# Seven small moves at the passage from projections to attention in a sparse graph attention layer

## The chip, the cores and the metric

The kernel runs on one core of a Trainium2 chip. The metric is the device time of one execution in microseconds (us); less is better. A core has TensorE (PE) for matrix products, VectorE (DVE), ScalarE (ACT) and GpSimd (POOL) for the rest, and a queue processor SyncE (SP). SP, ACT and POOL issue DMA transfers; the indirect ones (gathers and scatters by row numbers) are issued by POOL.

## The reference

One layer of graph attention over 4096 nodes of width 512, 8 heads of 64, then a feed-forward network and a last norm. The adjacency matrix is 4096 x 4096 of int32 and sparse: some 17 neighbours a row, the node itself among them.

```python
hs = layer_norm(x);  ht = layer_norm(h_target)           # with scale and bias, masked
q = (ht @ Wq + bq) / 8;  k = hs @ Wk + bk;  v = hs @ Wv + bv
logits = einsum('thd,shd->hts', q, k); logits = where(adj != 0, logits, -1e30)
ctx = einsum('hts,shd->thd', softmax(logits), v)
ht = layer_norm(ht + ctx @ Wo + bo)
out = _layernorm(x + ht + gelu(ht @ W1) @ W2)
```

## The kernel before

Rows lie in 32 tiles of 128. The kernel turns each adjacency row into a list of neighbours, sorts the rows by the number of neighbours so that rows of like degree share a tile, and then gathers the k|v rows of the neighbours. It has two stages.

*Stage 1* weaves three streams. `projections` normalizes x, multiplies it by Wk and Wv (L947, 16 pairs of tiles, n = 0 to 15) and writes each tile's k|v rows to a table in DRAM, `kvd` (L953, issued by ACT). Beside it `late_constants` makes small constants, one step at each n from 4 on; its last step, at n = 8, is a product of `rbc` and `wq` (L668) that corrects q's bias row `bqr` (L670, L671). `prepare` makes the lists of the first 16 adjacency tiles, part A: each quarter of a tile (512 KB) is loaded on SP (L714), turned into bytes by ACT (Sign, L733) and searched by DVE (L740, L742). Then `sort(0)` ranks the rows and POOL scatters the list records into DRAM (L871). `first_fronts` begins q for the first two (`EARLY`) sorted tiles. `fill` makes the lists of 7 further tiles (`FILL`).

*Stage 2* weaves four streams. `attention` goes over the sorted tiles in groups of `GROUPS`: 17 groups, the first and the last of one tile, the others of two. A sorted tile has a cap of neighbours (11 for tile 0, up to 39 for tile 15), and they are taken in steps `SG` of `S` = 3 slots. For each slot POOL gathers 128 k|v rows (L985) into a place of `ring`, up to 4 steps ahead (`request`, `issue`). DVE multiplies k by q (L1239) and sums by head (L1244), ACT takes Exp (L1248, L1257), DVE and ACT weight v (L1200 for the first two slots of a step of three, L1223 for the third, L1204 adds pairs), and PE adds the slots up in PSUM (L1211). `front(i)` prepares q of a tile: gather of target rows, norm (L1017), transposes (L1021, copies L1024), product with wq (L1031), bias (L1036). `finish` ends a tile: 1/sum, product with Wo (L1132), norm (L1150), transposes into `h2T` (L1159, L1163). `feed(g)` is the FFN of a group: W1 (L1344), gelu (L1347), W2 (L1353); it sleeps while `h2T` of its group is missing. `other_lists` makes the lists of the last 9 adjacency tiles and runs `sort(1)` for part B; it starts at `WAIT`. `weights` loads two quarters of W1 and W2.

`_weave` sets the order in which the program is written down: each stream yields costs in units, and the stream with the least sum goes next; a stream that yields None sleeps until another has gone. A group of two tiles costs 60 units in attention and 60 in its feed. A scheduler of the framework then makes each engine's queue: the written order is the priority, but work that is ready and finds its engine free may go ahead. `behind(ins)` (`tc.issue_after`) queues an instruction behind another of the same engine. For that purpose `front` has the tie L1013: a DVE step that reads what stage 1 or attention wrote last (`latest`) and passes on the two factors of the norm.

`prefetch(i)` loads the record of a sorted tile, on POOL for part A and on SP for most of part B, and requires that its part has been scattered (`done`). Tile 16 is the first of part B.

The ring has 17 places for part A and 20 for part B. In stage 1 its places 0 to 7 hold adjacency quarters, 8 to 11 rows of h_target, 12 to 16 rows of x; two further places (`wide`) hold the quarters of tiles from number 22 on.

Of the kernel before, what the change touches and what calls it, by code (L numbers as in the profile page):

```python
# [443 lines left out]
def adj_resnorm_kernel(  # L444
# [43 lines left out]
    NQ = 4  # L488
# [44 lines left out]
    with tc.tile_pool(name="keep", bufs=1) as keep:  # L533
# [17 lines left out]
        with ExitStack() as late:  # L551
# [146 lines left out]
                nc.vector.bn_aggr(mv, st)  # L698


            held, moms, factors, maxima = [], list(range(NT)), [], []
            mvh = wp.tile([P, NT, 2], F32, name="mvh")

# [16 lines left out]
            def edges(i):  # L720

                part = 1 if i >= NA else 0
                rec = Rs[part][:, i - PARTS[part][0], :]
                cand = lp.tile([P, SEG, 8], U16, name="cand", bufs=2)
                for h in range(NQ):
                    n = i * NQ + h
                    while len(adjs) < min(n + 2, NT * NQ):
                        adjs.append(quarter(*divmod(len(adjs), NQ)))
                    a, adjs[n] = adjs[n], None

                    sg = turn_of("signs", signs)
                    with behind(newest if i >= NA else []):
                        nc.scalar.activation(sg, a, AF.Sign, accum_out=dpart[:, i, h:h + 1])  # L733
                    ahead = min(n + DEEP - 1, n + 3 + n // 2)
                    while len(adjs) < min(max(n + 3, min(ahead, RINGED * NQ)), NT * NQ):
                        adjs.append(quarter(*divmod(len(adjs), NQ)))
                    yield 0.0 if i < NA else 0.7 if i < NA + FILL else 1.0
                    wd = sg.bitcast(U16)
                    with behind(logits):
                        nc.vector.tensor_tensor(wd, wd, lio, ALU.mult)  # L740
                    for s, (w0, w1) in enumerate(SEGS):
                        maxima[:] = [nc.vector.max(cand[:, h * SQ + s, :], wd[:, w0:w1]).ins]  # L742
                    if h == 1:
                        keep_rest()
                    if h % 2 and moms:
                        moments(moms.pop(0))
                    yield 1.8 if i < NA else 0.7 if i < NA + FILL else 1.0
                dec = dec_w
                nc.vector.tensor_single_scalar(dec[:, 0], cand, 255, op=ALU.bitwise_and)
                nc.vector.tensor_single_scalar(dec[:, 1], cand, 8, op=ALU.logical_shift_right)  # L750
                gid = lp.tile([P, 2 * SEG, 8], F32, name="gid")
                dec = dec.rearrange("p b s e -> p (b s) e")
                off = segoff.rearrange("p b q s -> p (b q s)")
                nc.vector.scalar_tensor_tensor(gid, dec, 0.0,
                                               off.unsqueeze(2).to_broadcast([P, 2 * SEG, 8]),
                                               op0=ALU.is_gt, op1=ALU.mult)
                nc.vector.scalar_tensor_tensor(gid, dec, 2.0, gid, op0=ALU.mult, op1=ALU.add)
                flat = gid.rearrange("p s e -> p (s e)")
                for r in range(RE // 8):
                    top = rec[:, E0 + r * 8:E0 + (r + 1) * 8]  # L760
                    nc.vector.max(top, flat)
                    if r + 1 < RE // 8:
                        nc.vector.match_replace(flat, top, flat, 0.0)
                held.append((rest_d[i * P:(i + 1) * P, :], flat))
                has = lp.tile([P, MAXE], F32, name="ehas")
                nc.vector.tensor_scalar(has[:, :RE], rec[:, E0:E0 + RE], 0.0, 0.0, op0=ALU.is_gt,
                                        op1=ALU.add, accum_out=cnt[:, i:i + 1])
                yield 2.4 if NA <= i < NA + FILL else 4.0
# [45 lines left out]
            def sort(part):  # L814
# [54 lines left out]
                for i in range(n):  # L869
                    with behind(issues):  # L870
                        ins = nc.gpsimd.indirect_dma_start(  # L871
                            out=recs_d[part][:, :],
                            out_offset=bass.IndirectOffsetOnAxis(ap=ranki[:, i:i + 1], axis=0),
                            in_=R[:, i, :], in_offset=None)

                    tc.declare_no_dep(ins.ins, group=f"scatter{part}", reason="other rows")
                    tc.add_to_no_dep_group(f"scatter{part}", ins.ins)
                    yield 3.0 if part else 1.3
                done.add(part)


# [107 lines left out]
            def prefetch(i):  # L989
                if i >= NT or i in recs:  # L990
                    return
                r0 = TILES[i][0]
                part = 1 if r0 >= PARTS[1][0] * P else 0
                assert part in done
                r0 -= PARTS[part][0] * P
                rec = sp.tile([P, E0 + MAXE], I32, name="rec", bufs=6)

                (nc.sync if part and i < NT - 4 else nc.gpsimd).dma_start(rec[:, :RW], recs_d[part][r0:r0 + P, :])
                recs[i] = rec

            def front(i, idle=0):


                rec = recs[i]
                tq = sp.tile([P, 2 * D], F32, name="tq", bufs=3)
                t = tq[:, :D]
                gather(t, h_target, rec[:, TGT:TGT + 1])
                for _ in range(max(idle, 1)):
                    yield


                m = rec[:, RST:RST + 2].bitcast(F32)
                tie = nc.vector.scalar_tensor_tensor(m, m, latest[-1], m, op0=ALU.bypass,  # L1013
                                                     op1=ALU.max)
                with tc.issue_after(tie.ins):
                    nc.vector.tensor_copy(tags[:, i, :], rec[:, DEG:TGT + 1])
                nc.scalar.activation(t, t, AF.Identity, bias=m[:, 1:2], scale=m[:, 0:1])  # L1017
                yield
                pt = ps.tile([P, KC, P], F32, name="t", bufs=2)
                for kc in range(KC):  # L1020
                    nc.tensor.transpose(pt[:, kc, :], t[:, kc * P:(kc + 1) * P], ident)  # L1021
                hT = tq[:, D:].rearrange("p (c t) -> p c t", c=KC)
                for kc in range(KC):
                    nc.scalar.activation(hT[:, kc, :], pt[:, kc, :], AF.Identity,  # L1024
                                         bias=b1r[:, kc:kc + 1], scale=s1c[:, kc:kc + 1])
                yield
                yield
                yield
                pq = ps.tile([P, D], F32, name="t", bufs=2)
                for kc in range(KC):  # L1030
                    nc.tensor.matmul(pq, hT[:, kc, :], wq[:, kc, :], start=kc == 0,  # L1031
                                     stop=kc == KC - 1)
                yield
                yield
                yield
                nc.vector.scalar_tensor_tensor(tq[:, :D], pq, HD ** -0.5, bqr,  # L1036
                                               op0=ALU.mult, op1=ALU.add)
                tqs[i] = tq
# [2 lines left out]

            SG = [(i, j0, min(S, cap - j0)) for i, (_, cap) in enumerate(TILES)
                  for j0 in range(0, cap, S)]
            kvs, rests, fronts = {}, {}, {}
            place = [11]
            for i, _, n in SG:
# [29 lines left out]
            def issue(k):  # L1076
# [3 lines left out]
                        begin(SG[k + d][0], d)  # L1080
                i, j0, n = SG[k]
                if j0 == 0:
                    prefetch(i + 2)
                    begin(i, 0)
                    if TILES[i][1] > RE:
# [85 lines left out]
            def first_fronts():  # L1171
# [4 lines left out]
                    step(fronts, i)  # L1176
                while not latest:
                    yield None
                while fronts:
                    go_on()  # L1180
                    yield 4.0

            def attention():
# [143 lines left out]
                    tc.add_to_no_dep_group("out", ins.ins)  # L1327

            def feed(g):
                while g not in h2Ts:  # L1330
                    yield None
                group, h2T = GROUPS[g], h2Ts.pop(g)
                nt = len(group)
                w = nt * P
# [62 lines left out]
                for g in gens:  # L1397
                    yield from g

            WAIT = 100.0  # L1400
            AHEAD = 4
            ADDS = 11
            HEAVY = 30
# [11 lines left out]
            def projections():  # L1415
                yield from _some(proj, G)
                consts = late_constants()
                for n in range(1, both):
                    if n > 3:
                        next(consts, None)  # L1420
                    yield from _some(proj, G)
                    if n in (8, 10):
                        load_quarter(wp2, n // 2 - 4)
# [47 lines left out]
                        load_quarter(pool, q + 2, nc.scalar)  # L1471

            def other_lists():
                for cost in ed:
                    yield 2.2 * cost
                keep_rest()
# [39 lines left out]
```

## Time and profile before

| | |
|---|---|
| median of 8 runs | 1792.59 us (1788.01 to 1797.17) |
| profiled execution | 1792.79 us, span 1791.0 us |
| PE busy | 1667.8 us, 93% of the span |
| DVE, ACT, POOL busy | 1425.4, 1239.9, 1022.9 us |
| gathers of k|v rows (L985) | 603, 1.32 us of POOL each |
| DMA | 461 MB, mean 257 GB/s |
| last k|v row issued, first gather of k|v rows | 276.01 us, 281.21 us |
| first FFN matmul | 344.91 us |

Times in the profile are microseconds from the start of the span. L12 is line 12 of the kernel. A stage's row gives the length, then the busy time of PE, PE's weight loads, DVE, ACT and POOL (with instruction counts), the granted clock of TensorE, the mean busy share of the 16 DMA engines, and GB/s. A wait names who waited (engine, tile, line), for whom, the sum, how often, and the longest. "Issue" is time in which the engine waited for nothing that the profile shows. POOL has 0.3 us of it ahead of nearly every gather. fp32 products count as two PE instructions each.

### The profile page before, as it was taken

To read this page: it belongs to the slowest core of one execution; us is meant where nothing else is said; L and a number is where in the kernel's file an instruction comes from. 1 tells how busy PE (TensorE), PEld (TensorE's weight loads), DVE (VectorE), ACT (ScalarE), POOL (GpSimd) and SP (SyncE) were. 2 spreads that over 40 slices of the span, in tenths; PEclk is the share of its full clock that TensorE was granted. 3 is DMA by queue.
4 is the path that set the end of the run, shared out by engine and by line. 5 is a ranking of instruction groups with operands and counts; after the bars stand their busy time and mean duration, and the time that the engine had idled before them with its cause. 6 is when DMAs were issued, how large, how long until landed. Compare 5 with 4: busy or idle time off the path is not lost. (4 is left out here: it accounts for less than half of the span.)

```text
span 1791.0 us, 22463 instructions
## 1 busy us (share of the span) xinstructions
PE 1667.8 (93%) x6850; PEld 1079.3 (60%) x6850; DVE 1425.4 (80%) x2449; ACT 1239.9 (69%) x3133; POOL 1022.9 (57%) x822
## 2 busy tenths in 40 slices
PE   7989985798999999997989999999999999999997
PEld 3444433556666766665656766666666666666665
DVE  6887786869888888996989888999797888988500
ACT  5776663558787888765777867787787677877511
POOL 1000155657456566787787787777677767764101
PEclk9999998898999999998999999999999999999999
DMA  9999978968678787777887788877668777775000
GB/s 351 361 384 358 365 241 300 338 230 286 250 251 300 275 312 276 248 233 228 284 288 279 263 296 296 288 251 264 231 219 280 241 255 232 241 251 198 19 5 26
DMA packets 141610, 461.00 MB, mean 257 GB/s; under 512 B 18036, under 2 KB 23048, under 8 KB 141480
## 3 DMA queue, kind: packets, MB, share of 16 engines
q0 software_dynamic: 96272, 342.33, 56.0%
q1 hardware_dynamic: 37392, 94.06, 14.8%
q10 hardware_dynamic: 7816, 23.08, 3.3%
q8 instruction: 57, 0.93, 0.2%
q14 instruction: 73, 0.60, 0.1%
HBM read 430.61 MB, written 28.79 MB: 257 GB/s over the span
## 5 line engine op out<-in xcount | busy, mean ns | idle before, releaser
L985 POOL DMA_INDIRECT kv<-kvd,rec x603 | 796.6, 1321 | 341.1 <-issue 130.3
L1344 PE MATMUL pf<-h2T,w 128*128 128x256 f32 (+1 forms) x2176 | 472.1, 371 | 7.2 <-ACT h2T L1163 3.8
L1353 PE MATMUL po<-w,gt 128*128 128x512 f32 x1024 | 463.7, 594 | 0.0
L1344 PEld LDWEIGHTS pf<-h2T,w 128*128 128x128 f32 x2176 | 391.2, 193 | 76.6 <-issue 22.3
L1239 DVE TENSOR_TENSOR kv<-kv,tq 128x1536 f32<-128x1536 f32 (+2 forms) x211 | 351.6, 1677 | 58.4 <-DMA kv<-kvd,rec 51.1
L1223 ACT ACTIVATE kv<-kv,pa 128x64 f32<-128x64 f32 x1520 | 391.0, 336 | 4.4
L1244 DVE TENSOR_REDUCE lg<-kv 128x24 f32<-128x1536 f32 (+2 forms) x211 | 350.5, 1669 | 0.6
L1353 PEld LDWEIGHTS po<-w,gt 128*128 128x128 f32 x1024 | 187.6, 191 | 194.5 <-issue 193.6
L1211 PE MATMUL cps<-ident,kv 128*128 128x128 f32 x1828 | 244.6, 280 | 52.7 <-DVE kv L1200 31.8
L1211 PEld LDWEIGHTS cps<-ident,kv 128*128 128x128 f32 x1828 | 217.8, 144 | 124.3 <-issue 48.4
L1200 DVE TENSOR_TENSOR kv<-kv,p 128x1024 f32<-128x1024 f32 (+1 forms) x211 | 251.6, 1194 | 24.8 <-ACT p L1248 23.1
L687 POOL TENSOR_TENSOR n_rs<-n_ve,mhalf 128x2 f32<-128x2 f32 (+2 forms) x51 | 50.5, 991 | 328.8 <-DVE n_ve L680 139.2
L733 ACT ACTIVATE kv<-kv 128x1024 uint8<-128x1024 int32 x128 | 134.5, 1053 | 53.9 <-DMA kv<-in_adj_dram 20.7
L1347 ACT ACTIVATE gt<-pf 128x512 f32<-128x512 f32 x128 | 76.4, 597 | 101.4 <-PE pf L1344 81.2
L1347 ACT ACT_TABLE_LOAD x110 | 141.1, 1283 | 1.8
L947 PE MATMUL pq<-wk,h2T 128*128 128x512 f32 x256 | 121.9, 620 | 6.1 <-ACT kv L949 2.5
L1132 PE MATMUL t<-wo,rb 128*128 128x512 f32 x256 | 119.3, 608 | 8.1 <-DVE rb L1122 8.1
L947 PE MATMUL pq<-wv,h2T 128*128 128x512 f32 x256 | 117.2, 601 | 4.6 <-DVE rbc L662 2.2
L1031 PE MATMUL t<-wq,tq 128*128 128x512 f32 x256 | 117.0, 601 | 1.3 <-ACT tq L1024 1.3
L742 DVE MAX8 cand<-kv 128x8 uint16<-128x171 uint16 (+1 forms) x384 | 108.5, 326 | 8.7 <-remote 3.8
L1248 ACT ACTIVATE p<-lg 128x24 f32<-128x24 f32 (+2 forms) x179 | 38.9, 217 | 77.5 <-DVE lg L1244 59.9
L947 PEld LDWEIGHTS pq<-wv,h2T 128*128 128x128 f32 x256 | 48.9, 192 | 68.3 <-issue 60.4
(163 smaller groups left out, 1597.6 us busy)
## 6 DMA issues: line engine op xcount, KB each, us to landing
kv<-in_adj_dram SPq DMA_DIRECT2D x128, 512.0 KB
kvd<-tq ACTq DMA_DIRECT2D x23, 512.0 KB
kv<-kvd,rec POOLq DMA_INDIRECT x603
kv<-in_L_gnn_h_target_dram SPq DMA_DIRECT2D x32, 256.0 KB
kv<-in_x_dram SPq DMA_DIRECT2D x15, 512.0 KB
kvd<-kv ACTq DMA_DIRECT2D x9, 512.0 KB
w<-in_L_gnn_W_dram SPq DMA_DIRECT2D x4, 1024.0 KB
w<-in_L_gnn_W_dram ACTq DMA_DIRECT2D x4, 1024.0 KB
```

The source lines that it names most:

```text
L733: nc.scalar.activation(sg, a, AF.Sign, accum_out=dpart[:, i, h:h + 1])
L947: nc.tensor.matmul(pkv, hT[:, kc, j * P:(j + 1) * P], w[:, kc, :], start=kc == 0, stop=kc == KC - 1)
L985: issues[:] = [nc.gpsimd.indirect_dma_start(out=dst, out_offset=None, in_=table[:, :], in_offset=bass.IndirectOffsetOnAxis(ap=idx, axis=0) ...
L1132: nc.tensor.matmul(pa, ct[:, c, :], wo[:, c, :], start=False, stop=c == KC - 1, skip_group_check=True)
L1200: nc.vector.tensor_tensor(v4, v4, p[:, j0:j0 + m, :].unsqueeze(3) .to_broadcast([P, m, H, HD]), ALU.mult)
L1211: nc.tensor.matmul(cps[:, c, :], kv[:, j, D + c * P:D + (c + 1) * P], ident, is_transpose=True, start=j0 + j == 0 and c == 0, stop=j0 + n ...
L1223: newest[:] = [nc.scalar.mul(v, v, pa[:, hd:hd + 1]).ins]
L1239: nc.vector.tensor_tensor(kv[:, :n, :D], kv[:, :n, :D], tq[:, :D].unsqueeze(1).to_broadcast([P, n, D]), ALU.mult)
L1244: logits[:] = [nc.vector.tensor_reduce(lg[:, :n, :], kv[:, :n, :D].rearrange("p j (h d) -> p j h d", h=H), AX.X, ALU.add).ins]
L1344: nc.tensor.matmul(pf[:, k, :], w1[(f0 + k) // KC][:, kc, (f0 + k) % KC * P:((f0 + k) % KC + 1) * P], h2T[:, kc, :w], start=kc == 0, stop= ...
L1347: nc.scalar.activation(gt, pf, AF.Gelu_apprx_tanh)
L1353: nc.tensor.matmul(po[j], gt[:, k, j * P:(j + 1) * P], w2[(f0 + k) // KC][:, (f0 + k) % KC, :], start=False, stop=f0 + k == FC - 1, skip_g ...
```

## The change

It has seven parts. (1, 2) The last step of `late_constants` is no longer run at n = 8; `first_fronts` runs it after its second turn, that is after the transposes of the first two q tiles. (3) For the first two tiles the norm follows the last k|v issue on ACT (`newest`), with no tie; their tag copies follow a DVE search instruction (`maxima`). (4) Tile 0's 11 slots are taken as 2, 3, 3, 3 instead of 3, 3, 3, 2; the ring places of later steps shift by one. (5) In stage 1 no adjacency quarter beyond tile 22 is loaded ahead; the first two quarters of tile 23 are loaded at the start of `other_lists`, at unit 94, and the lists go on 6 units later, at 100 as before. (6) The scatters of `sort(1)` come 4.5 units apart instead of 3.0; since they end later, `prefetch` returns where the part isn't done, and is asked at tile i + 1 as well. (7) A feed from group 4 on that has slept yields 3.0 units before it starts.

```diff
@@ edges
-                    while len(adjs) < min(n + 2, NT * NQ):
+                    top = (NA + FILL if i < NA + FILL else NT) * NQ
+                    while len(adjs) < min(n + 2, top):
...
-                    while len(adjs) < min(max(n + 3, min(ahead, RINGED * NQ)), NT * NQ):
+                    while len(adjs) < min(max(n + 3, min(ahead, RINGED * NQ)), top):
@@ sort
-                    yield 3.0 if part else 1.3
+                    yield 4.5 if part else 1.3
@@ prefetch
-                assert part in done
+                if part not in done:
+                    return
@@ front
+                if i < EARLY:
+                    with behind(newest):
+                        nc.scalar.activation(t, t, AF.Identity, bias=m[:, 1:2], scale=m[:, 0:1])
+                    with behind(maxima):
+                        nc.vector.tensor_copy(tags[:, i, :], rec[:, DEG:TGT + 1])
+                else:
                     (the tie, the tag copy and the norm as before)
@@ steps of attention
+            short = TILES[0][1] % S
+            if short:
+                SG[:-(-TILES[0][1] // S)] = [(0, 0, short)] + [(0, j0, S) for j0 in
+                                                              range(short, TILES[0][1], S)]
@@ issue
+                    prefetch(i + 1)
                     prefetch(i + 2)
@@ first_fronts
+                turns_done = 0
                 while fronts:
                     go_on()
+                    turns_done += 1
+                    if turns_done == 2:
+                        for _ in rest_consts[0]:
+                            pass
                     yield 4.0
@@ feed
+                slept = False
                 while g not in h2Ts:
+                    slept = True
                     yield None
+                if slept and g > 3:
+                    yield 3.0
@@ projections
-            WAIT = 100.0
+            WAIT = 94.0
...
                 consts = late_constants()
+                rest_consts.append(consts)
                 for n in range(1, both):
                     if n > 3:
-                        next(consts, None)
+                        if n < 8:
+                            next(consts, None)
@@ other_lists
+                for _ in range(2):
+                    adjs.append(quarter(*divmod(len(adjs), NQ)))
+                yield 6.0
```

More of the change, by code (lines that the diff above doesn't have):

```diff
@@ L698, in stats @@
                 nc.vector.bn_aggr(mv, st)
+            rest_consts = []
             held, moms, factors, maxima = [], list(range(NT)), [], []
@@ L1012, in front @@
                 m = rec[:, RST:RST + 2].bitcast(F32)
[L1013 to L1017, printed above, removed]
+                if i < EARLY:
[4 more added lines that the diff above has]
+                else:
+                    tie = nc.vector.scalar_tensor_tensor(m, m, latest[-1], m, op0=ALU.bypass,
+                                                         op1=ALU.max)
+                    with tc.issue_after(tie.ins):
+                        nc.vector.tensor_copy(tags[:, i, :], rec[:, DEG:TGT + 1])
+                    nc.scalar.activation(t, t, AF.Identity, bias=m[:, 1:2], scale=m[:, 0:1])
                 yield
```

## The prediction

> **What bounds the kernel now.** I read the page first: PE is busy 93% of the span, so the question is where the other 123 us are. Its line of 40 slices (44.8 us each) shows one dip.
>
> ```profile
> PE   7989985798999999997989999999999999999997
> ...
> PEclk9999998898999999998999999999999999999999
> DMA  9999978968678787777887788877668777775000
> ```
>
> Slices 7 and 8 (269 to 358 us) have PE at 5 and 7 tenths: the passage from projections to attention. Slice 19, 806 us on, is a smaller dip. The table of busy time by stage puts numbers on both. Its columns are PE, PEld, DVE, ACT and POOL busy, granted clock, DMA share and GB/s.
>
> ```profile
> 140.00:240.00 100.00, 100.00 (x278) 47.23 (x277) 79.54 (x316) 67.94 (x127) 19.07 (x16) 1.00 0.97 352
> 240.00:276.00 36.00, 30.39 (x71) 12.76 (x69) 26.48 (x103) 21.25 (x40) 12.37 (x16) 0.95 0.67 222
> 276.00:345.00 69.00, 38.76 (x153) 25.22 (x153) 49.13 (x63) 26.84 (x94) 46.62 (x38) 0.78 0.92 339
> 345.00:720.00 375.00, 358.84 (x1698) 252.22 (x1699) 313.30 (x525) 288.99 (x742) 230.72 (x186) 0.98 0.78 271
> 720.00:960.00 240.00, 214.49 (x925) 146.19 (x925) 209.52 (x248) 168.19 (x469) 191.06 (x148) 0.95 0.77 258
> ```
>
> The projections are PE's (100.00 of 100). The passage is nobody's: PE idles 30 of 69 us there, and its 39 busy us are slow ones, at a clock of 0.78. From 720 to 960 POOL is the full engine: 191 us busy, and 148 instructions with the 0.3 us of issue ahead of nearly each make 235 of 240. I then followed the passage in the timeline (start, length, instruction, and in brackets the idle time before it with its releaser):
>
> ```profile
> 147.38 3.60 PE L668 MATMUL pq<-wq,rbc 128*128 128x512 f32 x8
> ...
> 276.01 0.33 ACTq L953 DMA_DIRECT2D kvd<-kv  x1
> ...
> 277.61 0.20 DVE L1013 SCALAR_TENSOR_TENSOR rec<-rec,kv 128x2 f32<-128x2 f32 x1
> ...
> 277.85 1.52 ACT L1017 ACTIVATE tq<-tq,rec 128x512 f32<-128x512 f32 x2 [1.87 <-DVE rec L1013]
> ...
> 278.71 1.97 PE L1021 MATMUL t<-ident,tq 128*128 128x128 f32 x8 [3.36 <-ACT tq L1017]
> ...
> 281.21 0.97 POOL L985 DMA_INDIRECT kv<-kvd,rec  x1 [23.48 <-PE t L1021]
> 281.43 8.99 PE L1031 MATMUL t<-wq,tq 128*128 128x512 f32 x16 [0.75 <-ACT tq L1024]
> ...
> 287.10 0.69 DVE L1036 SCALAR_TENSOR_TENSOR tq<-t,bqr 128x512 f32<-128x512 f32 x1 [8.27 <-PE t L1031]
> ...
> 289.77 1.76 DVE L1239 TENSOR_TENSOR kv<-kv,tq 128x1536 f32<-128x1536 f32 x1 [1.98 <-DMA kv<-kvd,rec]
> ```
>
> The last k|v row is issued to DRAM at 276.01, the first row is gathered back at 281.21, and the first product waits at 289.77 for gathered rows, not for q, which was ready at 287.79. The first FFN matmul comes at 344.91; from there PE has work beside attention. For the later dip, PE's and POOL's waits of 820 to 862 us:
>
> ```profile
> PE cps L1211 <- DVE kv L1204: 12.4, 1, 12.4
> ...
> POOL kv L985 <- PE cps L1211: 1.7, 3, 1.1
> ```
>
> **The change, part by part.** The sum is made against the profiled execution, 1792.79 us (span 1791.0 and 1.8 around it), 0.2 above the median 1792.59. The measurement can tell about 0.2%, 3.6 us, from no change.
>
> *1. q's bias product leaves the projections.* L668 holds PE from 147.38 to 150.82, where the next product starts: 3.43 us in a stretch where PE has no idle time. I take 3.4 us off. The bounds are 0 and -3.6: the stretch 240 to 276 leaves PE 5.6 us idle behind ACT and DVE, and could swallow it. The two DVE steps on bqr (0.67 and 0.42 us) leave too, and find DVE idle for 8.27 us before L1036.
>
> *2. Where it goes.* Behind the last matmul of the projections PE idles 3.36 us, then 0.75 more before L1031. The product (3.60 us at full clock) fits if it is queued there at once, and costs about 0; it then even keeps PE from cooling. If it lies behind the transposes L1021, it runs as L1031 does now: 16 instructions in 8.99 us, 0.56 each, so 8 take 4.5 (7.2 at 0.50 throughout). Less the 0.75 idle and the 1.98 that DVE waits anyway, that is at most +4.5. The work is ready long before and q's rows need ACT first, so I take the first place: 0, with 0 to +4.5 for the range. A gain beyond that is excluded since the gathers end the wait. The granted clock is 0.50 from 280 to 284 us. The Trainium skill, TensorE: Matmul & The Clock Gate, Part 1, has half rate after an idle window of about 3.4 us and until a busy one of that length; by it a product queued first would leave L1021 and L1031 at full rate and q some 2 us earlier, where the gathers end the wait and the sum stays, and one queued second would take the whole 7.2 and make the sum -2.1.
>
> *3. Norm of the first two q row tiles.* The norm L1017 no longer waits for the DVE step L1013: it follows the issue at 276.01 on ACT, at 276.34 instead of 277.85, so 1.5 us earlier. Behind it on ACT stand only L1024's eight, which want the same. Alone this gains 0, because q is 1.98 us early already; it makes room for part 4. The tag copies go behind another DVE instruction and nobody waits for them.
>
> *4. Tile 0 as 2, 3, 3, 3.* The first product needs two gathers instead of three. POOL issues them 1.25 us apart (281.21, 282.49, 283.74), and 0.5 MB at the 297 GB/s of these microseconds takes 1.75. DVE starts up to 1.9 us earlier, with q ready in time by part 3. DVE's total for the tile stays: 1.08 us less on the first group (1.21 for 1.75, twice), 1.08 more on the last. But tile 1's groups wait for DMA again (L1239 1.67, 1.10 and 2.49 us between 313 and 326), and the gather stream behind those starts no earlier. I take -0.7 of 0 to -1.9.
>
> *5. Two adjacency loads fewer before the kvd row.* They are 0.5 MB each, issued on SP from 272.09. The row's write takes 5.2 us from its issue to the first gather, beside about 0.4 MB of theirs; at 400 GB/s that is 1 us, and the releaser named is PE's L1021, which part 3 moves by 1.5. The bounds are 0 and -2.0. The loads, issued 6 weave units before their Sign, have SP idle from 278 to 391 us to themselves. Program order is only a wish: the memset L642 runs at 1.0 us, its DMA L643 at 80.1. So they may stay where they were. I take -0.5. [...]
>
> *6. Scatters of the second list, 4.5 for 3.0 units.* By the weave's costs they span units 358 to 406 and will span 358 to 430. FFN group 0 starts at unit 58.9 and at 344.91 us, group 4 at 302.4 and 689.45, so a unit is 1.41 us. Each scatter takes POOL 1.0 us and 0.3 of issue. Spread, five of 16 leave the stretch in which PE stalled for 12.4 us. But POOL waited there only 1.7 us for a free slot, and it stays full to 960: what is not scattered before 862 is scattered after. A full engine finishes no sooner. The bounds are what POOL idled (-5) and a scatter or two more in a denser tile (+2). I take -1.5. The record of tile 16 is now asked for at tile 15 (unit 437) instead of 14 (407), behind the last scatter at 430; tile 16's gathers begin at 484, 66 us later, so nobody waits. It is queued on SP, where only rare adjacency and list transfers stand.
>
> *7. Three units of rest after a sleeping feed.* By the costs feeds 4, 9, 12 and 14 sleep now; with the rest only 4 and 9 do, and the last ends at the same unit (1031). At feed 4 the FFN's first matmul waits 2.87 us for h2T; 3 units (4.2 us) of attention go ahead of it. That gains up to 2.9, or costs up to 4.2 if attention has nothing ready for PE. I take -0.5.
>
> Sum: -3.4 + 0 + 0 - 0.7 - 0.5 - 1.5 - 0.5 = -6.6, so 1786.2 us. Next late after this is still the gather stream of tiles 0 and 1, at a DMA share of 1.0.
>
> **The rivals.**
> *The edits are absorbed.* The product's 3.4 us vanish in the 5.6 us that PE idles before 276, the adjacency loads are issued where they were, POOL's full stretch keeps its length: 0 to -3, so about 1791. For it: DVE is busy 26.48 of 36 us there, and the full POOL. Against it: PE has no idle time for 100 us, and its matmuls run close from 260 on.
> *The product goes behind the transposes.* +4.5 against -3.4 and parts 4 to 7 halved: about 1792.
> *Slower: scatters among the dense tiles.* The tiles of caps 23 and 24 and then 39 give POOL more gathers per microsecond of FFN; 5.3 scatters, each with 1.0 to 1.3 us and issue, about 8 us, come where DVE already waits for gathers (9.2 us at 823). It decides if the stall at 832 stays although scatters left it, so that they only add a second: -6.6 + 1.5 + 8 = +3 or more, about 1796. For it: POOL has no free slot to refill from until 960. Against it: the same full queue, in which order alone adds nothing.
>
> **How the numbers follow.** Forecast 0.55 (own range 1778 to 1789), absorbed 0.18, product behind 0.10, scatters 0.17. Faster by over 0.2% (below 1789.0) is the forecast and a little of the absorbed: 0.58. Within 0.2%: 0.22. Slower: 0.20. The range goes from all gains at their low ends (-3.4 - 1.9 - 2.0 - 5.0 - 2.9 = -15.2, or 1777.6) to 2 us beyond the dear rival: 1777 to 1798.
>
> **What would show it.** Right: no L668 between projections, 8 matmuls of wq and rbc just behind the last of L947, L1021 without the 3.36 us, L1239 first on 128x1024 and within 13 us of the last row's issue, feed 4 without its 2.87 us wait, and the first FFN matmul near 340. Wrong: that matmul still at 345; the stall after 820 undiminished or followed by another before 960; a new wait of PE or DVE for tile 16's record.

## The result and the profile after

The changed kernel takes 1786.41 us (median of 25 runs, 1779.38 to 1795.21) against 1794.45 us of the kernel before beside it (67 runs). The ratio is 0.9956, 95% interval 0.9945 to 0.9968: 7.9 us less (5.7 to 9.8; a thousandth is 1.79 us). The forecast was 1786.2 us, and -6.6 for the sum. The time came out, with luck: the kernel before is 1.7 us slower here than the execution that the forecast started from, the gain 1.3 us more than the sum, and most of the terms are wrong, as the experiments show.

The profiled execution took 1797.88 us (span 1796.1), the longest of the changed kernel's executions, while that of before (1792.79 us) lay near its median. So the two profiles are compared by what happens inside them, not by where each ends. The changed kernel's lines lie 1 to 23 further down: L947, L953, L985, L1021, L1031, L1036, L1211, L1239 and L1344 of before are L949, L955, L987, L1030, L1040, L1045, L1230, L1258 and L1367. In the experiments they shift by a few lines more or less; the operand names say which is meant.

The page after, the rows of 40 slices:

```profile
PE   7999885889999999798888999999999999999997
...
PEclk9999997899999999899999999999999999999999
...
DMA  9999978968778797667778797877677777765000
```

Slices 7 and 8 have 5 and 8 tenths (5 and 7 before), at a lower clock; the small dip of slice 19 has gone to slice 17 and to four slices of 8 (19 to 22). The stages of after (length; PE, PEld, DVE, ACT, POOL busy; clock; DMA share; GB/s):

```profile
140.00:240.00 100.00, 95.37 (x257) 44.33 (x256) 76.90 (x302) 64.54 (x122) 19.12 (x16) 0.98 0.97 346
240.00:276.00 36.00, 30.89 (x77) 13.48 (x76) 26.92 (x106) 21.87 (x41) 11.40 (x15) 1.00 0.66 216
276.00:345.00 69.00, 43.67 (x184) 30.16 (x183) 51.03 (x60) 26.73 (x96) 47.61 (x39) 0.70 0.93 344
345.00:720.00 375.00, 361.97 (x1696) 252.47 (x1695) 318.38 (x538) 290.96 (x751) 233.88 (x189) 0.99 0.79 275
720.00:960.00 240.00, 204.78 (x876) 140.49 (x875) 194.97 (x226) 160.96 (x436) 184.72 (x139) 0.93 0.73 241
```

From 276 to 345 PE is busy 4.9 us more than before (43.67 for 38.76), part of it the moved product and all at a lower clock (0.70 for 0.78); from 345 to 720 it is 3.1 us more, from 720 to 960 9.7 less. And from 140 to 240, where the product has left, PE is no longer busy throughout: 95.37 of 100. The passage in the timeline of after:

```profile
271.28 2.68 SPq L715 DMA_DIRECT2D kv<-in_adj_dram  x2
...
274.13 3.60 PE L668 MATMUL pq<-wq,rbc 128*128 128x512 f32 x8
...
274.95 0.33 ACTq L955 DMA_DIRECT2D kvd<-kv  x1
...
275.38 1.52 ACT L1018 ACTIVATE tq<-tq,rec 128x512 f32<-128x512 f32 x2 [0.46 <-ACT kv L951]
...
277.57 1.04 PE L1030 MATMUL t<-ident,tq 128*128 128x128 f32 x8
...
279.77 7.13 PE L1040 MATMUL t<-wq,tq 128*128 128x512 f32 x16 [1.16 <-ACT tq L1033]
...
280.62 0.97 POOL L987 DMA_INDIRECT kv<-kvd,rec  x1 [22.73 <-DMA rest_d<-gid]
...
287.09 1.22 DVE L1258 TENSOR_TENSOR kv<-kv,tq 128x1024 f32<-128x1024 f32 x1 [2.83 <-DMA kv<-kvd,rec]
```

All is where the forecast put it: the product in the idle time behind the projections, the norm right behind the last row's issue, no wait at the transposes, a first attention product of 1024 columns 12.14 us behind that issue (13.76 before). Only the loads of adjacency tile 23 are where they were, 3.7 us ahead of the last k|v row. The rest of the page's dip, PE's waits from 720 to 960:

```profile
PE cps L1230 <- DVE kv L1223: 14.4, 5, 8.3
PE t L1030 <- DVE kv L854: 11.3, 1, 11.3
PE cps L1230 <- issue: 9.4, 2, 7.6
```

The stall of 12.4 us is gone as one piece; there are others in its stead.

### The profile page after: what moved, and what is told of

It is laid out like the page before. It is cut to its first block, busy times and chain, and to the rows that moved or that the text cites. A ratio compares the mean times of both kernels' runs of the same rounds, so it can differ in the third digit from the quotient of the medians.

```text
span 1796.1 us, 22466 instructions
## 1 busy us (share of the span) xinstructions
PE 1668.6 (93%) x6850; PEld 1078.4 (60%) x6850; DVE 1423.4 (79%) x2447; ACT 1237.5 (69%) x3131; POOL 1016.5 (57%) x822
## 5 line engine op out<-in xcount | busy, mean ns | idle before, releaser
L987 POOL DMA_INDIRECT kv<-kvd,rec x603 | 792.8, 1315 | 342.3 <-issue 129.0
L1367 PE MATMUL pf<-h2T,w 128*128 128x256 f32 (+1 forms) x2176 | 473.0, 370 | 4.2 <-ACT h2T L1177 4.2
L1367 PEld LDWEIGHTS pf<-h2T,w 128*128 128x128 f32 x2176 | 390.7, 192 | 73.1 <-issue 22.4
L1258 DVE TENSOR_TENSOR kv<-kv,tq 128x1536 f32<-128x1536 f32 (+2 forms) x211 | 351.9, 1677 | 72.2 <-DMA kv<-kvd,rec 41.1
L1230 PE MATMUL cps<-ident,kv 128*128 128x128 f32 x1828 | 247.8, 282 | 50.1 <-issue 18.6
L1230 PEld LDWEIGHTS cps<-ident,kv 128*128 128x128 f32 x1828 | 218.5, 145 | 126.0 <-issue 59.9
L949 PE MATMUL pq<-wk,h2T 128*128 128x512 f32 x256 | 121.7, 619 | 2.7 <-ACT kv L951 1.9
L949 PE MATMUL pq<-wv,h2T 128*128 128x512 f32 x256 | 117.3, 601 | 7.0 <-ACT kv L951 4.6
L1040 PE MATMUL t<-wq,tq 128*128 128x512 f32 x256 | 118.2, 605 | 4.2 <-ACT tq L1033 4.2
```

What stands on the lines that cost most here:

```text
L949: nc.tensor.matmul(pkv, hT[:, kc, j * P:(j + 1) * P], w[:, kc, :], start=kc == 0, stop=kc == KC - 1)
L987: issues[:] = [nc.gpsimd.indirect_dma_start(out=dst, out_offset=None, in_=table[:, :], in_offset=bass.IndirectOffsetOnAxis(ap=idx, axis=0) ...
L1230: nc.tensor.matmul(cps[:, c, :], kv[:, j, D + c * P:D + (c + 1) * P], ident, is_transpose=True, start=j0 + j == 0 and c == 0, stop=j0 + n ...
L1258: nc.vector.tensor_tensor(kv[:, :n, :D], kv[:, :n, :D], tq[:, :D].unsqueeze(1).to_broadcast([P, n, D]), ALU.mult)
L1367: nc.tensor.matmul(pf[:, k, :], w1[(f0 + k) // KC][:, kc, (f0 + k) % KC * P:((f0 + k) % KC + 1) * P], h2T[:, kc, :w], start=kc == 0, stop= ...
```

## The experiments

Each kernel was timed beside the kernel before on the same chip; ratios are to that. "Before" below is the kernel before.

**Four parts of the change alone.** *Parts 1 to 4 on before:* product, norm, tile 0 as in the change's diff.

> The kernel before with the product moved, the early norm and the first tile as 2, 3, 3, 3 (parts 1 to 4), nothing else. My theory: the whole gain of the change lies in these, since after them the first FFN matmul came 3 us earlier: -3 to -5 us against the kernel before, ratio about 0.998, first FFN matmul 2.5 to 3.5 us before that of the kernel before, and L1239 first on 128x1024 within 13 us of the last k|v issue. The stall of PE between 820 and 862 us stays above 8 us. Rival (absorbed): 0 to -1 us, the first FFN matmul earlier but the next full stretch of POOL swallows it, since POOL issues the same gathers. Second rival: this part holds nearly all 8 us, -7 to -9.

Measured: 0.9955 (0.9935 to 0.9975), or -8.1 us, which is the second rival and more than my theory had. The three other parts, each alone:

```diff
-                    yield 3.0 if part else 1.3
+                    yield 4.5 if part else 1.3          (with the return and prefetch(i + 1))
```

> The kernel before with the scatters of the second list 4.5 units apart (part 6), nothing else. My prediction's term: -1.5 us; a full POOL finishes no sooner, so between 720 and 960 POOL's busy time stays near 191 us, and the 12.4 us wait of PE on L1211 shrinks but returns in pieces. First rival, from the changed kernel's trace (stage 720 to 960 with 10 us less of PE busy and the stall at 832 gone): -4 to -6 us. Second rival: the scatters among dense tiles cost, +3 us or more, and the stall at 832 stays above 8 us.

Measured: 1.0006 (0.9987 to 1.0025).

```diff
+                if slept and g > 3:
+                    yield 3.0
```

> The kernel before with the 3.0 units of rest after a feed that slept (part 7), nothing else. My prediction's term: -0.5 us, and the 2.87 us wait of feed 4's first W1 matmul for h2T is gone. Rival: the rest only moves the wait to attention, 0 within 1 us, with a new wait of PE on L1211 of 2 to 3 us in its place; the other end is +4 us, where attention has nothing ready.

Measured: 1.0003 (0.9981 to 1.0024).

```diff
-                    while len(adjs) < min(n + 2, NT * NQ):
+                    while len(adjs) < min(n + 2, top):  (the second loop alike, WAIT 94, two loads at the lists' start)
```

> The kernel before with the adjacency quarters beyond tile 22 asked for at unit 94 (part 5), nothing else. From the changed kernel's trace, where SP still issued two loads at 271 us: 0 within 1 us, two 512 KB loads still issued by SP before 280 us and 5 to 6 us from the last k|v issue to the first gather. Rival: they move behind 300 us, that distance falls to 3.5 to 4.5 us, and the time by 1 to 2 us.

Measured: 1.0000 (0.9983 to 1.0017). SP still issued the two loads, at 270.37. So parts 1 to 4 hold all of the gain, and none of the other three gives anything alone that can be told (each within 4.5 us of 0).

**The passage taken apart.** *Product alone:*

> The kernel before with the product alone moved (parts 1 and 2; norm with its tie and first tile 3, 3, 3, 2 as before). My prediction: -3.4 us, and 0 to +1 for its new place, since the norm waits for the tie as before. Theory from the traces (the kernels with feed or adjacency alone began their first W1 product 4 us earlier by chance, and had given that back at the fifth tile): a start of attention earlier by 3 us alone is lost again, 0 to -1 us, and the Wo product of tile 5 is within 1 us of its place before (525.8 us). Rival: -3 to -4 us, and that product 3 us earlier.

Measured: 1.0000 (0.9981 to 1.0020). *Tile 0 as 2, 3, 3, 3 alone:*

> The kernel before with the first tile's slots alone as 2, 3, 3, 3 (part 4). My prediction's term: -0.7 us of 0 to -1.9. Theory from the traces: the first group is not what gains, the shifted ring places of all later steps are; between 390 and 436 us PE waits 4 to 7 us less, and the tile's gain is kept: -4 to -6 us. Rival: 0 to -1 us, PE's idle time between 390 and 440 stays near 10 us.

Measured: 0.9967 (0.9949 to 0.9985), -5.9 us. *Norm and tile 0, without the product:*

> The kernel before with the early norm and the first tile as 2, 3, 3, 3 (parts 3 and 4), product in its old place. My prediction's terms: 0 and -0.7, and with the product's -3.4 missing about 4 us slower than parts 1 to 4 together. Theory of the shifted ring: -5 to -8 us, as parts 1 to 4 together (-8.1). Rival: -1 to -2 us, with L1239 first on 128x1024 2 to 3 us earlier and nothing kept of it after the fifth tile.

Measured: 0.9976 (0.9957 to 0.9994), -4.3 us. *Product and norm, without tile 0:*

> The kernel before with the product moved and the early norm (parts 1 to 3), first tile 3, 3, 3, 2 as before. My prediction's terms: -3.4 and 0, so about -3.4 us. Theory of the shifted ring: 0 to -1.5 us, with the Wo product of tile 5 within 1.5 us of its place before (525.8 us). Rival: -7 to -8 us, the first tile's division does nothing and an earlier start is what counts.

Measured: 0.9979 (0.9962 to 0.9997), -3.8 us. The last is more than my theory had. The sign that I had named for it and for the product alone, the Wo product of tile 5, came at 519.63 and 522.20 us for 525.82, early as the rivals had it, though the product alone gains nothing: one execution's place in time tells little. Tile 0's division is the one edit that is shown to gain by itself. The product gains nothing that can be told alone (-3.4 to +3.6 us). With the norm it has -3.8 (-6.8 to -0.5); the norm alone was not run, so how these two share it stays open.

*Where tile 0's division gains.* The stage 390 to 440 us, first before, then product alone, then 2, 3, 3, 3 alone:

```profile
390.00:440.00 50.00, 39.64 (x176) 27.88 (x174) 43.19 (x76) 40.35 (x107) 36.53 (x27) 0.86 0.81 290
```

```profile
390.00:440.00 50.00, 40.49 (x187) 29.18 (x186) 44.98 (x80) 40.99 (x110) 34.95 (x25) 0.93 0.82 305
```

```profile
390.00:440.00 50.00, 44.32 (x192) 31.53 (x191) 46.83 (x99) 42.44 (x115) 34.52 (x28) 0.90 0.89 322
```

With the new division PE does 4 to 5 us more here, DVE 2 to 4, and the DMA engines move 322 GB/s for 290 to 305. The changed kernel has the same signature (43.81 of PE, 323 GB/s). This is 110 us behind the first group. Is it the short first group at all? *Tile 0 as 3, 2, 3, 3,* on before (shown against 2, 3, 3, 3):

```diff
-                SG[...] = [(0, 0, short)] + [(0, j0, S) for j0 in range(short, ...)]
+                SG[...] = [(0, 0, S), (0, S, short)] + [(0, j0, S) for j0 in range(S + short, ...)]
```

> The kernel before with the first tile's slots alone as 3, 2, 3, 3. From the third step on the places in the ring are those of 2, 3, 3, 3, but the first group has three gathers to wait for. Theory (the later order gains, not the first group): -4 to -6 us as with 2, 3, 3, 3 alone (-5.9), first gather to first product 8 to 9 us as before (8.56), DMA share of 390 to 440 us near 0.9 and PE busy there about 44 us. Rival (the short first group gains): 0 to -1 us, DMA share near 0.8 and PE busy 40 to 42 us there.

Measured: 0.9965 (0.9949 to 0.9981), -6.3 us. The first product waits for three gathers again:

```profile
285.28 1.76 DVE L1243 TENSOR_TENSOR kv<-kv,tq 128x1536 f32<-128x1536 f32 x1 [2.32 <-DMA kv<-kvd,rec]
```

That is 8.17 us behind the first gather (8.56 before, 6.47 in the changed kernel), and the gain is whole. Its stage 390 to 440:

```profile
390.00:440.00 50.00, 44.67 (x206) 32.06 (x205) 49.14 (x101) 44.43 (x122) 36.53 (x29) 0.93 0.91 333
```

So the short first group is not the cause. What 3, 2, 3, 3 and 2, 3, 3, 3 share is that tile 0 ends on a full group and that steps 5 to 19, those of tiles 1 to 3, lie elsewhere in the ring (from the 20th on the places are those of before). Which of the two it is was not separated, and how it gains is not shown.

**What sets the first gather.** Product alone, the passage in its timeline:

```profile
264.28 3.60 PE L948 MATMUL pq<-wv,h2T 128*128 128x512 f32 x8
267.40 1.06 ACT L734 ACTIVATE kv<-kv 128x1024 uint8<-128x1024 int32 x1 [5.77 <-DMA kv<-in_adj_dram]
267.71 3.60 PE L668 MATMUL pq<-wq,rbc 128*128 128x512 f32 x8
...
268.58 2.06 SPq L715 DMA_DIRECT2D kv<-in_adj_dram  x2
...
270.19 1.06 ACT L950 COPY kv<-pq 128x512 f32<-128x512 f32 x2
...
271.28 0.33 ACTq L954 DMA_DIRECT2D kvd<-kv  x1
...
278.12 0.98 POOL L986 DMA_INDIRECT kv<-kvd,rec  x1 [18.39 <-DMA rest_d<-gid]
```

PE is done with the projections at 267.7, where the product starts. That is no earlier than in the three kernels with the product in its old place that were profiled on the same chip: 266.9 (2, 3, 3, 3), 267.7 (norm and tile 0) and 268.3 (3, 2, 3, 3). What the product leaves free is gone before. Its stage 140 to 240, and in it a product of `sort(0)` (L864) with what leads up to it:

```profile
140.00:240.00 100.00, 96.72 (x264) 45.21 (x263) 77.99 (x306) 65.92 (x124) 19.50 (x17) 1.00 0.97 352
```

```profile
204.46 1.29 DVE L697 BATCH_NORM_STATS2 n_st<-kv 128x6 f32<-128x512 f32 x2 [3.47 <-DMA kv<-in_x_dram]
...
207.27 0.81 ACT L909 ACTIVATE kv<-kv,n_nm,n_rs 128x512 f32<-128x512 f32 x1 [7.96 <-DVE n_nm L692]
...
211.33 0.42 DVE L741 TENSOR_TENSOR kv<-kv,lio 128x512 uint16<-128x512 uint16 x1 [3.49 <-ACT kv L734]
...
216.03 0.93 DVE L853 TENSOR_TENSOR_SCAN kv<-one_c,cps 128x384 f32<-128x384 f32 x1
...
217.02 0.32 PE L864 MATMUL cps<-oh,lower 128*128 128x384 bf16 x1 [2.98 <-DVE kv L853]
```

Before, this product runs at 218.18 with no wait:

```profile
218.18 0.33 PE L863 MATMUL cps<-oh,lower 128*128 128x384 bf16 x1
```

PE comes to it earlier and waits for a scan of DVE (L853). The scan stands behind DVE's search of adjacency quarters, DVE waits for ACT's Sign of these, ACT stands behind the norm of rows of x (L909), and DVE had waited 3.47 us for the load of such rows (4.41 before), at a DMA share of 0.97. In the seven profiles with the product moved PE is busy 95.0 to 96.7 of these 100 us and waits for the scan for 1.3 to 3.0; in the seven with it in its old place it is busy 97.4 to 100.0, and two of them wait for the scan (1.7 and 2.6 us).

Then ACT waited 5.77 us for a quarter of adjacency tile 22, and the two copies of the last k|v row stand behind its Signs: they run at 270.19, and the row is issued 3.57 us behind the start of L668 (0.82 in the changed kernel's profile, where ACT waited less). This is not the product's doing either: ACT waited 4.2 to 5.6 us there in the three kernels named. Last, the row follows the next two loads by 2.70 us (3.92 before) and takes 6.84 us to the first gather (5.20 before). In thirteen profiles the first gather came 7.9 to 10.2 us behind the issue of these two loads, though the row's issue lay 2.2 to 5.2 us behind it.

The trace names another releaser for that gather, the write of a list (`rest_d`). By the semaphores in the traces it landed 0.2 to 0.3 us behind the row's own write in all thirteen, so it moves little; in the four kernels with the old norm where q's transposes on PE are named, these came 0.0 to 0.4 us later still.

*The changed kernel with the two loads truly late:*

```diff
+                    with tc.issue_after(exps[-1]):      (exps: attention's last Exp, on ACT)
+                        adjs.append(quarter(*divmod(len(adjs), NQ), nc.scalar))
```

> The changed kernel with the first two adjacency quarters of tile 23 issued by ACT behind the Exp that attention had last, so that they can't start ahead of the last k|v row. In ten kernels the first gather came 8.2 to 10.2 us after the issue of these two loads, wherever the last k|v row's issue lay (2.2 to 5.2 us behind it). Theory: the two loads set the first gather. It then comes 2.5 to 4 us behind the last k|v issue, the product's 3.4 us arrive, and the time falls by 2 to 3 us beyond the changed kernel's ratio of 0.9956, to 0.994 or 0.9945. Rival: the k|v write itself takes 4.4 to 6.8 us, the distance stays above 4 us, and the ratio stays at 0.9956. Second rival: the first gather comes earlier, but nothing of it is kept after the fifth tile (ratio 0.9956).

```profile
273.72 0.33 ACTq L955 DMA_DIRECT2D kvd<-kv  x1
...
277.20 0.97 POOL L987 DMA_INDIRECT kv<-kvd,rec  x1 [14.96 <-PE t L1030]
```

The distance is 3.48 us, and the list's write is issued too late (276.87) to be waited for. The row's own write landed 2.66 us behind its issue by the trace's semaphores, 4.28 before and 5.92 in product alone: these loads did lengthen the write. But the row itself is issued at 273.72, 3.51 behind the start of L668 (270.21), since the Signs ahead of its copies waited 5.07 us for loads of tile 22, as in product alone. And the ratio is 0.9984 (0.9966 to 1.0002), no better than the changed kernel, rather worse. Nor is the first gather, at 277.20, earlier than in most of the other kernels on that chip (273.86 in one, 276.28 to 278.12 in five). So the shorter write brought nothing that can be told. The two loads, on ACT at 378 us, come into a stretch where PE then waits 5.4 us for `rb` (L1136), which may be their price; that was not tried apart.

**POOL's full stretch.** *The second lists earlier:*

```diff
-                    yield 2.2 * cost
+                    yield 1.8 * cost                    (and scatters 3.0 apart again)
```

> The changed kernel with the second lists taken 1.8 units a step for 2.2 and their scatters 3.0 units apart again, so that the scatters end some 50 units (70 us) earlier, in a stretch where POOL has idle time. Theory (720 to 960 is bound by POOL): POOL's busy time there falls by about 10 us, PE's waits on L1230 there by 5 or more, and the time by 3 to 5 us beyond 0.9956. Rival: POOL is not what ends the stretch; the gathers' own transfers are, and the ratio stays at 0.9956 or rises, with new waits of PE between 345 and 720 where DVE takes the lists in less time.

Measured: 1.0060 (1.0036 to 1.0084), +10.7 us. The scatters end near 790 us, and PE is indeed busier where they were (stages 820 to 910 and 910 to 1035):

```profile
820.00:910.00 90.00, 80.78 (x348) 56.35 (x347) 76.11 (x91) 60.43 (x158) 65.50 (x52) 0.94 0.80 273
910.00:1035.00 125.00, 120.00 (x552) 83.81 (x551) 115.37 (x113) 99.30 (x287) 96.46 (x76) 0.97 0.84 285
```

The price stands from 345 to 720, in PE's waits:

```profile
PE cps L1230 <- DVE kv L1219: 16.3, 3, 9.9
```

(0.9 in the changed kernel.) There DVE has the lists in less time, and PE waits for its products, as the rival had it. POOL's busy time from 720 to 960 did not fall (184.86 us for 184.72). The rival's other half, that the gathers' transfers end POOL's stretch, is not shown.

**Part 7 undone** in the changed kernel:

> The changed kernel without the 3.0 units of rest (part 7 undone). The wait of PE on L1030 for the scan L854 of the second list (11.3 us in the changed kernel, 5.4 with part 7 alone, 7.1 with late loads) stood in the three profiles that have part 7 with the lists at 2.2 units, and in none of the nine without part 7. Theory: part 7 makes it; without it that wait is under 4 us, feed 4 waits near 2.9 us for h2T, and the ratio is 2 to 5 us below the changed kernel's 0.9956, near 0.994. Rival: the wait goes, but the next full stretch of POOL takes the time instead, and the ratio stays at 0.9956 (parts 1 to 4 alone had 0.9955).

Measured: 0.9989 (0.9971 to 1.0007), -2.0 us. PE's wait for the scan is gone, as the theory said:

```profile
PE cps L1230 <- DVE kv L1223: 11.6, 2, 9.2
PE cps L1230 <- DVE kv L1219: 8.9, 1, 8.9
PE pf L1363 <- ACT h2T L1177: 5.2, 2, 2.7
PE t L1142 <- DVE kv L866: 3.1, 1, 3.1
```

But the kernel is slower than with part 7, by 5.9 us (about 2 to 10). So both theory and rival miss: beside part 6 the rest is worth something that it isn't worth alone. The profiles show one thing that it does in each kernel with it and 2.2 units (changed, part 7 alone, late loads): PE's wait of 4.1 us for `tq` at the transposes of `finish`, between 1140 and 1340 us, present in before and with part 7 undone, falls to 0.7 or 0.8. That isn't 5.9, and the scan costs part of it; the rest is open.

## Why the prediction was right, and where it wasn't

The time was right and the sum near by luck: a term mis-sized at too little and others at too much cancelled. Most of what the rival of absorbed edits said came true (the product's time vanished, the loads stayed, the scatters gained nothing); tile 0 alone kept it from being right. Point by point:

*1. Product out of the projections, -3.4: not shown.* Alone it gave 0 (-3.4 to +3.6). The step that failed is "a stretch where PE has no idle time". PE had none because the product filled it: without it PE waits up to 3.0 us, 70 us later, at the sort's product for DVE, at the end of a chain that begins with a load. The stage's row had the sign of it, a DMA share of 0.97 beside PE's 100.00, and I called the stretch PE's alone. I had named the stretch from 240 to 276 as what could swallow the gain, and it is lost before that.

*2. Its place: right.* It begins 3.43 us behind the start of the last k|v product, with no gap. L1030 then takes 1.04 us for 1.97, L1040 7.13 for 8.99. The Trainium skill, TensorE: Matmul & The Clock Gate, Part 1, has half rate after an idle window and full rate after a busy one; these rows agree with it, and q's earlier end was worth nothing by itself, as forecast.

*3. Norm: right as to its place* (0.43 us behind the issue's start, 1.84 before). Its worth of 0 was not tested alone.

*4. Tile 0, -0.7 of 0 to -1.9: wrong, -5.9 (-9.1 to -2.7).* The mechanism that I costed is there: the first product comes 2.1 us nearer to the first gather. By the fifth product this is gone (it starts 25.84 us behind the first gather before, 26.34 after), also as forecast. What failed is the scope: I costed the division at the group that it shortens, and not what it moves behind it. The gain lies at 390 to 440 us and needs no short first group (3, 2, 3, 3: -6.3).

*5. Adjacency, -0.5: it was 0,* the bound that I had named (they may stay where they were). I had costed the loads at 1 us of the write; taken away for good, they shortened it from 5.20 or 5.67 us to 3.48, but not the kernel.

*6. Scatters, -1.5: wrong in mechanism.* Alone +1.1 (-2.3 to +4.5). The stages 820 to 910 and 910 to 1035, before and with part 6 alone:

```profile
820.00:910.00 90.00, 76.55 (x341) 52.77 (x340) 75.43 (x79) 60.12 (x163) 72.02 (x60) 0.92 0.80 273
910.00:1035.00 125.00, 117.73 (x541) 82.71 (x540) 108.32 (x114) 95.95 (x268) 94.21 (x73) 0.97 0.81 277
```

```profile
820.00:910.00 90.00, 79.17 (x345) 54.29 (x344) 74.28 (x78) 61.70 (x169) 70.44 (x57) 0.94 0.76 252
910.00:1035.00 125.00, 112.65 (x507) 78.63 (x506) 103.69 (x111) 91.82 (x259) 92.40 (x75) 0.95 0.81 278
```

PE gains 2.6 us in the first and loses 5.1 in the second. Its stall between 820 and 862 us is still 9.2 us (12.4 before). In the second all four kernels with part 6 have 110.7 to 112.7 of PE, all ten without it 115.0 to 120.0. And my step "so nobody waits" for the record of tile 16 fell. POOL, part 6 alone, behind the last scatter at 889.12 and the records' load on SP at 893.20:

```profile
898.19 2.73 POOL L985 DMA_INDIRECT kv<-kvd,rec  x1 [3.59 <-DMA rec<-rec]
```

Before, those records are loaded at 862.10 and no gather waits for them; the changed kernel waits 3.60 us, part 7 undone 3.07. I had worked it out from the weave's units (430 and 484), a wish as to order, when the engine that is full asks for the next tile's rows ahead. A wait for tile 16's record was one of the signs of being wrong that I had named. How much of the 5.1 us it makes is not shown, and the change as a whole is not slower by 3 us or more, as the slower rival had it.

*7. Feed, -0.5: alone +0.5 (-3.4 to +4.3).* The wait of feed 4 did not go: 2.86 us in the changed kernel and 3.44 with part 7 alone, for 2.87.

Of the signs that I named, "first FFN matmul near 340" was no sign: it came at 341.77, but part 5 and part 7 alone had it at 340.51 and 340.94 with a passage as before, and a ratio of 1.000. One execution's place in time varies by more than 4 us.

## What to carry to other kernels

An edit of a step's size changes the buffers and the queue order of every later step: cost it there too, and test it apart from the effect that it was made for (a variant that keeps the order and gives up the effect, as 3, 2, 3, 3). An engine may be without idle time only because of the instruction that you take out: find the next thing on it that another engine feeds, and ask when that comes (here a scan that hangs on loads). When a stream is spread out, look for who loads what it wrote, and on which engine that one waits.

## What the runs showed of the hardware

The write of a 512 KB k|v row tile, issued 2.2 to 5.2 us behind a megabyte of loads from another queue, took 3.55 to 7.21 us from issue to the first gather that reads it, on the whole longer the closer it followed, (3.55 at 5.2 us), and 3.48 us with no such loads ahead. And kernels that differ by an edit of no worth (part 5, part 7) had the first FFN matmul up to 4.4 us apart in one execution each.
